# A list-scheduled attention pass in which every operation's place comes from a table instead of a formula

## The chip, the cores and the metric

The kernel runs on one core of one Trainium2 chip. The metric is the device time of one execution in microseconds (us). Five engines of the core work side by side, each through its own instructions in order, and wait for each other on semaphores: TensorE (PE in the profile, with its weight loads as PEld), VectorE (DVE), ScalarE (ACT), GpSimd (POOL) and SyncE (SP), which here issues most of the DMA transfers.

## The reference, cut to what matters

The input is four images of 192 channels and 128 x 128 pixels, in float32. Two layers follow each other. The first is a channel attention; the change doesn't touch it. The second is an attention over dilated neighbourhoods:

```python
pe = conv3x3_depthwise(x, pos_w)                    # 192 channels
x = x + pe + pos_b
q, k, v = split(einsum('oc,bchw->bohw', qkv_w, x))  # three groups of 64 channels each
for dil in (1, 2, 3):                               # a group for each dilation, 2 heads of 32 channels
    scores = sum_d(q * k[3x3 neighbours at distance dil]) / sqrt(32)
    attn = softmax(scores over the 9 neighbours)
    out[group] = sum over the 9 neighbours of attn * v[neighbour]
out = einsum('oc,bchw->bohw', proj_w, out)
```

Borders of k and v are reflected.

## The kernel before, in words

The kernel has three stages. A first pass projects the input and convolves it, a middle stage forms the channel attention's small matrices, and `second_pass` (line 740 on) does the rest: the last 1x1 product of the first layer and the whole second layer. The change concerns the second pass alone.

The second pass works on 64 blocks. A block is four image rows (512 pixels) of a pair of images; 32 blocks make one pair. Each block n goes through these steps:

- **Projection** (`plan_h`): six loads (SP, `loads`, lines 790 and 793), then for each of three tiles m three accumulated matmuls (`h_product`, line 803; m = 2 uses half of TensorE's columns), and an eviction by ACT (`h_evict`, line 807) into a ring of 12 rows, `hboth` and `hring2`.
- **Position convolution** (`plan_conv`): the `centre` tap by ACT into PSUM (pool `pa`, one buffer; line 846), seven taps by DVE that accumulate there (`tap`, line 858), the last of which writes `y`; an eighth neighbour by ACT (`moved`, line 870) that POOL adds (`moved_sum`, line 875). The remaining 64 channels go by nine ACT products (`side`, line 882), two accumulating DMAs that POOL issues (`side_rows`, line 894) and two POOL sums (lines 902 and 905).
- **Keys and values** (`plan_kv`): three pairs of products. A pair's first part (line 945) takes two buffers of the PSUM pool `pc`, the second part (line 948) uses half of TensorE's rows; four evictions by ACT (line 958) go to the rings `kring` (12 rows) and `vring` (16 rows), with reflected columns (lines 962 and 963).
- **Scores** (`plan_scores`): for each of three groups a query in PSUM (pool `q`, one buffer; lines 1000 and 1003), three products by DVE with the shifted keys (`prod`, line 1011), and sums over channels by TensorE (`pick_sums`, line 1022, in a quarter of TensorE's columns).
- **Softmax** (`plan_softmax`): `evicted_scores` (1065), `by_pixel` (1072), `top` (1075), `below` (1079), `exponential` (1082), `total` (1086 and 1087), `divide` (1091), a split of the weights into three bfloat16 parts (1095 to 1105), and a DMA transpose (`weights`, 1110) to `e_sb`.
- **Mixing** (`plan_mixed`): for each of 27 pairs of a group g and a neighbour t TensorE spreads the weights over channels (`expand`, line 1146, two PSUM buffers `ex`), DVE multiplies with the shifted values (`term`, line 1152), and POOL adds (`term_sum`, line 1155; 24 of them, since the first term of a group starts the accumulator). Then come the output products (`out_product`, lines 1164 and 1168, again in `pc`), evictions by ACT (line 1171) and stores by SP.

`pc` has two buffers and serves projection, key/value and output products in turn. `hold` says from which operation to which a buffer is in use.

Nothing of this is issued where it is written. Each step calls `Schedule.add` with an engine, a *rank*, a cost and the operations it comes after. `Schedule.order` (line 60 on) then walks through time with these costs: whenever an engine is free, it takes the ready operation of lowest rank. Ranks count in blocks, so `n + 2` is two blocks after the block's own number. On TensorE an operation whose tile shape differs from the last one's costs `CHANGE` more and has `CHANGE_RANK` added to its rank. The result is one fixed order for every engine; the costs live only in this planning, on the chip the engines follow the order and wait where they must. Buffers of a pool are handed on in order of rank as well. In the kernel before, the ranks are formulas in the code, such as `n + 2 + (j + 0.9) / 8` for tap j, and `t0 + (NT * g + t) / 27` for the mixing.

Of the kernel before, what the change touches and what calls it, by code (L numbers as in the profile page):

```python
# [24 lines left out]
RING = 12  # L25
RING_V = 16
SPARE = 3
NT = 9
# [6 lines left out]
class Schedule:  # L35
# [4 lines left out]
    LATENCY, CHANGE, CHANGE_RANK = 0.2, 0.13, 0.05  # L40

    def __init__(self):
        self.ops, self.pools = [], {}

# [10 lines left out]
    def order(self):  # L55
        import heapq

        for (_, bufs), held in self.pools.items():
            held.sort(key=lambda h: (h[0]["rank"], h[0]["seq"]))
            for i, (first, _) in enumerate(held):  # L60
                if i >= bufs:
                    first["after"] += held[i - bufs][1]
                if i and held[i - 1][0] is not first:
                    first["first"].append(held[i - 1][0])
        for op in self.ops:
            op["left"] = len(op["after"]) + len(op["first"])
            for o in op["after"]:
                o["users"].append(op)
            for o in op["first"]:
                o["issued"].append(op)  # L70
        events, ready, free, shape, out = [], {}, {}, None, []
        for op in self.ops:
            ready.setdefault(op["engine"], [])
            free[op["engine"]] = 0.0
            if not op["left"]:
                heapq.heappush(events, (0.0, op["seq"]))

        def release(op, now):
            op["left"] -= 1
            op["ready"] = max(op.get("ready", 0.0), now)  # L80
            if not op["left"]:
                heapq.heappush(events, (op["ready"], op["seq"]))

        while events:
            now = events[0][0]
            while events and events[0][0] <= now:
                seq = heapq.heappop(events)[1]
                if seq >= 0:
                    ready[self.ops[seq]["engine"]].append(self.ops[seq])
            for engine, ops in ready.items():  # L90
                if not ops or free[engine] > now:
                    continue
                change = lambda o: bool(o["shape"]) and o["shape"] != shape
                op = min(ops, key=lambda o: (o["rank"] + self.CHANGE_RANK * change(o), o["seq"]))
                ops.remove(op)
                end = now + op["cost"] + self.CHANGE * change(op)
                shape = op["shape"] or shape
                free[engine] = end
                heapq.heappush(events, (end, -1))
                out.append(op)  # L100
                for o in op["issued"]:
                    release(o, now)
                for o in op["users"]:
                    release(o, end + op["latency"] * (o["engine"] != engine))
        assert len(out) == len(self.ops)
        self.span = max(free.values())
        return out
# [29 lines left out]
class Stage:  # L137


    def __init__(self, ctx, tc, prefix, sbuf, psum, pools={}):  # L140
        self.nc, self.bufs = tc.nc, {**sbuf, **psum}
        self.schedule, self.tiles, self.written, self.readers = Schedule(), {}, {}, {}
        self.pools = dict(pools)
        for n, k in self.bufs.items():
            if n in pools:
                continue
            space = dict(space=bass.MemoryType.PSUM) if n in psum else {}
            self.pools[n] = ctx.enter_context(tc.tile_pool(name=prefix + n, bufs=k, **space))
# [19 lines left out]
    def repeat(self, ring, kind, m, n, size, rank):  # L168

        if n * RB % size:  # L170
            return
        run = lambda: self.nc.scalar.copy(ring[m][:, size : size + SPARE, :], ring[m][:, 0:SPARE, :])
        after = self.written[kind, m, n] + self.readers.get((kind, m, n - size // RB), [])
        self.written[kind, m, n].append(self.schedule.add("ACT", rank, 0.55, (run,), after))
# [20 lines left out]


# [550 lines left out]
def second_pass(tc, x, w2, xv_p, mix1, mix2, biases, v_dram, v2_dram, out):  # L747
# [4 lines left out]
    with ExitStack() as ctx:  # L752
# [9 lines left out]
            dict(xv=xv_p),  # L762
        )
# [13 lines left out]
        for r in hring:  # L777
            nc.gpsimd.memset(r[:, :, 0 : W + 2 : W + 1], 0.0)

# [34 lines left out]
        def plan_h(n):  # L814
            loaded = [
                [add("SP", n - 0.5 + 0.05 * j, 0.1, (loads, n, j, im), latency=6.0) for im in range(2)]
# [3 lines left out]
            for m in range(3):  # L820
                t = n + 0.65 + 0.11 * m
                ops = [
                    add("PE", t + 0.03 * j, 0.86, (h_product, n, m, j), shape=FULL if m < 2 else COLS)
                    for j in range(3)
                ]
# [6 lines left out]
                ev = add("ACT", t + 0.1, 0.7, (h_evict, n, m), [ops[2]])  # L832
                fill("h", m, n, RING, ev)
                repeat(hring, "h", m, n, RING, t + 0.11)
# [72 lines left out]
        def plan_conv(n):  # L907
            prev = first = add("ACT", n + 2, 1.25, (centre, n), latency=0.3)
            for m in range(2):
                read("h", m, n, 0, first)  # L910
            for j, t in enumerate(AROUND[:7]):
                prev = add("DVE", n + 2 + (j + 0.9) / 8, 1.28, (tap, n, t, j == 6), [prev])
# [4 lines left out]
            mv = add("ACT", n + 2.5, 1.2, (moved, n, AROUND[7]))  # L917
            for m in range(2):
                read("h", m, n, 0, mv)
            both = add("POOL", n + 2.9, 2.4, (moved_sum, n), [mv, two])  # L920
            hold("moved", mv, both)
            firsts, sums = {}, []
            for j, ty in enumerate((1, 0, 2)):
                for tx in range(3):
                    sd = add("ACT", n + 2 + 0.3 * j + 0.08 * tx, 0.72, (side, n, ty, tx), firsts.get(ty, [])[-1:])
                    read("h", 2, n, ty - 1, sd)
                    firsts.setdefault(ty, []).append(sd)
                if j:
                    after = [firsts[1][-1], firsts[ty][-1], *sums[-1:]]
                    sums.append(add("POOL", n + 2.25 + 0.3 * j, 1.2, (side_rows, n, ty), after, latency=6.0))  # L930
                    hold("side", firsts[ty][0], sums[-1])
            for tx in (1, 2):
                sums.append(add("POOL", n + 2.95 + 0.02 * tx, 1.28, (side_sum, n, tx), sums[-1:]))
# [33 lines left out]
        def plan_kv(n, y):  # L967
            used = []
            for pair, t in ((0, n + 3), (1, n + 4.4), (2, n + 4.15)):
                a = add("PE", t, 1.72, (kv_product, n, pair, 0), [y[2]], FULL)  # L970
                b = add("PE", t + 0.03, 0.86, (kv_product, n, pair, 1), [a] + y[3], ROWS)
# [3 lines left out]
                for im in range(2):  # L975
                    for e, (kind, g) in enumerate(groups):
                        ev = add("ACT", t + 0.05 + 0.01 * im, 0.6, (kv_evict, n, pair, im, e, kind, g), [b])
                        evs[e].append(ev)
                    hold("pc", a, *(ops[-1] for ops in evs))
                for e, (kind, g) in enumerate(groups):  # L980
# [3 lines left out]
                    bd = add("ACT", t + 0.07, 0.45, (reflect, n, kind, g), evs[e] + evs[e][0]["after"])  # L984
                    written[kind, g, n] = evs[e] + [bd]
                    repeat(ring, kind, g, n, size, t + 0.08)
# [43 lines left out]
        def plan_scores(n, y):  # L1030
            t0 = n + 4.65
            prods, used, picks = [], [], []
            for g in range(NG):
                a = add("PE", t0 + (NT * g + 0.1) / 27, 0.86, (query, n, g, 0), [y[2]], COLS)
                b = add("PE", t0 + (NT * g + 0.11) / 27, 0.86, (query, n, g, 1), [a] + y[3], FULL)
                used += [a, b]
                mine = []
                for ty in range(3):
                    op = add("DVE", t0 + (NT * g + 3 * ty + 0.5) / 27, 1.75, (prod, n, g, ty), [b])
# [4 lines left out]
            for row in range(7):  # L1044
                of = prods[4 * row // 3 : min(4 * row + 3, NG * NT - 1) // 3 + 1]
                op = add("PE", of[-1]["rank"] + (2.5 + 0.1 * row) / 27, 0.86, (pick_sums, n, row), of, QUADS)
# [65 lines left out]
        def plan_softmax(n, picks):  # L1112
            t0 = n + 5.65
            chain = [picks[-1]]

            def then(engine, t, cost, run, shape=None):
                op = add(engine, t0 + t, cost, (run, n), chain[-1:], shape)
# [3 lines left out]
            s = then("ACT", 0.045, 0.6, evicted_scores)  # L1121
            hold("sc", picks[0], s)
            st = then("PE", 0.05, 0.9, by_pixel, FULL)
            hold("s_sb", s, st)
            mx = then("DVE", 0.05, 0.6, top)
            lo = then("DVE", 0.05, 0.6, below)
            hold("sc", st, lo)
            hold("mx", mx, lo)
            then("ACT", 0.1, 0.55, exponential)
            sm = then("DVE", 0.14, 1.3, total)  # L1130
            dv = then("POOL", 0.16, 0.95, divide)
            hold("sm", sm, dv)
            p0 = then("ACT", 0.19, 0.55, part0)
            then("POOL", 0.21, 1.05, rest)
            then("ACT", 0.24, 0.55, part1)
            p2 = then("POOL", 0.26, 1.05, part2)
            hold("e", lo, p2)
            w = then("SP", 0.3, 0.3, weights)
# [44 lines left out]
        def plan_mixed(n, w):  # L1183
            t0 = n + 6.1
            sums, spreads = [], []
            for g in range(NG):
                exs, prev = [], None
                for t in range(NT):
                    u = t0 + (NT * g + t) / 27
                    exs.append(add("PE", u - 0.6 / 27, 0.25, (expand, n, g, t), [w], FULL))  # L1190
                    tm = add("DVE", u + 0.7 / 27, 0.62, (term, n, g, t), exs[-1:])
# [5 lines left out]
                    prev = add("POOL", u + 1.2 / 27, 1.27, (term_sum, n, g, t), [tm, prev])  # L1197
# [5 lines left out]
            for m in range(2):  # L1203
                ops = []
                for g in range(NG):
                    after = [sums[g][1]] + ops[-1:]
                    ops.append(
                        add(
                            "PE",
                            n + 7.25 + 0.07 * m + 0.01 * g,  # L1210
                            0.86,
                            (out_product, n, m, g),
                            after,
                            FULL if m else ROWS,
                        )
                    )
                used += ops
                for e in range(2 - m):
                    ev = add("ACT", ops[-1]["rank"] + 0.02, 0.6, (out_evict, n, m, e), ops[-1:])
                    hold("pc", ops[0], ev)  # L1220
                    st = add("SP", ev["rank"] + 0.02, 0.3, (store, n, m, e), [ev], latency=5.0)
# [154 lines left out]
```

## Time and profile before

| | |
|---|---|
| median of 3 runs | 4564.9 us (4564.49 to 4565.8) |
| the profiled execution | 4564.56 us, of which the span from first to last instruction is 4562.7 us |
| busy share of the span | PE 97%, DVE 86%, ACT 55%, POOL 74% |
| mean granted TensorE clock | 0.987 |
| first sum of the mixing (line 1155) | 1768.9 us |
| last such sum begins | 4548.4 us |
| DMA | 608.93 MB, 133 GB/s on average |

The page cuts the span into 40 slices and gives the busy share of each in tenths:

```profile
PE   9999999899999989999999999999999999999986
...
DVE  7998889755455547899999999999999999999996
ACT  7888888633233345555555555555555555555531
POOL 6777788611111115888989999998998989999897
PEclk9999999999999989999999999999999999999997
```

The first seven slices are the first pass, the next eight the middle stage, and from the fifteenth on the second pass runs. There PE, DVE and POOL are all at eight or nine tenths, ACT at five. A busy share includes the ends of instructions that overlap the next one, so three engines at nine tenths don't say which of them sets the pace. The mixing is the largest part of the second pass in number:

```profile
L1155 POOL TENSOR_TENSOR acc<-acc,term 128x512 f32<-128x512 f32 x1536 | 1977.4, 1289 | 211.9 <-DVE term L1152 135.5
L1152 DVE TENSOR_TENSOR term<-ex,vring 128x512 f32<-128x512 f32 (+2 forms) x1596 | 1007.3, 661 | 65.8 <-PE ex L1146 38.9
L1011 DVE TENSOR_TENSOR prod<-q,kring 128x1536 f32<-128x1536 f32 (+1 forms) x600 | 1008.3, 1686 | 31.7 <-ACT kring L963 13.8
```

After the shapes and the count stand the busy time in us, the mean of one instruction in ns, and the engine's idle time just before them with what ended most of it.

### The profile page before, as it was taken

The numbers are of one execution on the slowest core, as the hardware profiler recorded it, in microseconds if no ns is written. First come the engines' busy times: TensorE is split into PE (matmuls) and PEld (weight loads), VectorE is DVE, ScalarE is ACT, GpSimd is POOL, SyncE is SP. The second block draws the span as 40 slices with busy tenths as digits, with TensorE's granted clock in tenths as the row PEclk, the third lists the DMA queues.
The fourth block names the chain that finished last, engine by engine and source line by source line (L and its number), as shares of the span: only waits on it lengthen the run. The fifth ranks groups of instructions, "written<-read, shape, count | busy, mean of one in ns | idle before, by whom it ended". The sixth has DMA issues, their size and how long they took to land.

```text
span 4562.7 us, 64190 instructions
## 1 busy us (share of the span) xinstructions
PE 4416.8 (97%) x20608; PEld 1602.8 (35%) x20608; DVE 3907.4 (86%) x5556; ACT 2506.2 (55%) x4794; POOL 3354.2 (74%) x3343
## 2 busy tenths in 40 slices
PE   9999999899999989999999999999999999999986
PEld 3333333345544532333333333333333333333321
DVE  7998889755455547899999999999999999999996
ACT  7888888633233345555555555555555555555531
POOL 6777788611111115888989999998998989999897
PEclk9999999999999989999999999999999999999997
DMA  8777787678677734443444443444434444344311
GB/s 271 241 242 232 244 256 242 192 164 178 150 167 169 167 89 97 99 99 97 101 98 93 105 103 91 106 96 101 101 90 108 98 100 101 92 109 99 78 44 28
DMA packets 483951, 608.93 MB, mean 133 GB/s; under 512 B 136528, under 2 KB 318364, under 8 KB 483616
## 3 DMA queue, kind: packets, MB, share of 16 engines
q1 hardware_dynamic: 464160, 504.94, 40.6%
q0 software_dynamic: 19456, 99.89, 11.3%
q8 instruction: 166, 2.72, 0.3%
q14 instruction: 169, 1.38, 0.1%
HBM read 277.72 MB, written 201.33 MB: 105 GB/s over the span
## 4 chain that ended last, share of the span: by engine, by line
PE 71%; DVE 14%; issue 6%; POOL 6%; DMA 2%; ACT 1%; POOLq 0%; SPq 0%; DVEq 0%; ACTq 0%
PE pc L576 11%; PE ph L803 9%; PE pu L293 7%; PE ex L1146 6%; PE sc L1022 6%; DVE prod L1011 5%; DVE term L1152 5%; POOL acc L1155 4%; PE pu L298 4%; PE gram L648 4%; PE po L1168 3%; PE po L1164 3%; PE pkv L945 3%; PE pu L426 2%; PE q L1000 2%
## 5 line engine op out<-in xcount | busy, mean ns | idle before, releaser
L1155 POOL TENSOR_TENSOR acc<-acc,term 128x512 f32<-128x512 f32 x1536 | 1977.4, 1289 | 211.9 <-DVE term L1152 135.5
L1152 DVE TENSOR_TENSOR term<-ex,vring 128x512 f32<-128x512 f32 (+2 forms) x1596 | 1007.3, 661 | 65.8 <-PE ex L1146 38.9
L1011 DVE TENSOR_TENSOR prod<-q,kring 128x1536 f32<-128x1536 f32 (+1 forms) x600 | 1008.3, 1686 | 31.7 <-ACT kring L963 13.8
L363 POOL TENSOR_TENSOR v_True<-v_True,side 128x512 f32<-128x512 f32 (+1 forms) x512 | 647.9, 1267 | 168.8 <-ACT side L352 141.1
L340 DVE SCALAR_TENSOR_TENSOR pa<-vboth,dwv,pa 128x1024 f32<-128x1024 f32 (+1 forms) x448 | 574.3, 1282 | 76.8 <-ACT pa L333 54.3
L1146 PE MATMUL ex<-e_sb,spread 108*128 108x512 bf16 x1728 | 596.2, 387 | 45.2 <-DVE acc L1152 21.3
L858 DVE SCALAR_TENSOR_TENSOR pa<-hboth,posw,pa 128x1024 f32<-128x1024 f32 (+1 forms) x384 | 489.5, 1275 | 59.0 <-ACT pa L846 45.1
L576 PE MATMUL pc<-u,band 64*64 64x508 f32 (+1 forms) x4608 | 517.5, 590 | 1.4 <-ACT ring L322 1.4
L563 POOL COPY band<-band 64x384 f32<-64x384 f32 x192 | 96.7, 504 | 561.3 <-DMA band<-in_bands 484.8
L1022 PE MATMUL sc<-prod,pick 128*32 128x512 f32 x3456 | 484.1, 607 | 4.1 <-DVE e L1079 2.8
L589 DVE BATCH_NORM_STATS2 stats<-pc 128x6 f32<-128x128 f32 x1440 | 303.3, 283 | 141.3 <-ACT conv L585 141.1
L1146 PEld LDWEIGHTS <-spread 108*128 108x128 bf16 x1728 | 149.0, 98 | 723.7 <-issue 692.2
L945 PE MATMUL pkv<-y,wkv 128*128 128x512 f32 x768 | 389.0, 618 | 8.1 <-ACT kring L958 2.5
L882 ACT ACTIVATE side<-hring,posw 128x512 f32<-128x512 f32 x512 | 335.2, 710 | 102.1 <-DMA side<-side 79.8
L803 PE MATMUL ph<-xv,mix 128*128 128x512 f32 (+1 forms) x1024 | 383.4, 606 | 5.4 <-DMA xv<-v_dram 4.9
L585 ACT COPY conv<-pc 128x512 f32<-128x512 f32 x384 | 211.4, 587 | 295.4 <-PE pc L576 288.8
L293 PE MATMUL pu<-xt,wx 128*128 128x512 f32 x768 | 365.3, 612 | 7.6 <-DMA xt<-in_x 7.6
L352 ACT ACTIVATE side<-ring,dwv 128x512 f32<-128x512 f32 (+1 forms) x512 | 350.6, 736 | 15.1 <-POOL v_True L363 14.3
L958 ACT COPY kring<-pkv 64x512 f32<-64x512 f32 x384 | 223.2, 581 | 221.7 <-PE pkv L948 210.5
L576 PEld LDWEIGHTS pc<-u,band 64*64 64x64 f32 x4608 | 188.4, 133 | 302.3 <-issue 282.1
L1171 ACT COPY o<-po 128x512 f32<-128x512 f32 x192 | 106.2, 588 | 304.5 <-PE po L1164 203.8
L958 ACT COPY vring<-pkv 64x512 f32<-64x512 f32 x384 | 223.4, 582 | 45.4 <-PE pkv L948 35.7
(164 smaller groups left out, 5961.0 us busy)
## 6 DMA issues: line engine op xcount, KB each, us to landing
qk_dram<-us SPq DMA_DIRECT2D x192, 512.0 KB
u<-qk_dram SPq DMA_DIRECT2D x384, 256.0 KB
side<-side POOLq DMA_DIRECT2D x124, 768.0 KB, 5.8
xt<-in_x SPq DMA_DIRECT2D x64, 512.0 KB
v_dram<-v_False SPq DMA_DIRECT2D x64, 512.0 KB
xv<-in_x SPq DMA_DIRECT2D x128, 256.0 KB
xv<-v_dram SPq DMA_DIRECT2D x128, 256.0 KB
out<-o SPq DMA_DIRECT2D x128, 256.0 KB
```

Source lines behind the costliest of these rows:

```text
L293: mm(pu, wx[:, mt * 128 : (mt + 1) * 128], tiles["xt", n][:, im, :], start=True, stop=False)
L340: nc.vector.scalar_tensor_tensor(by_row(to[:, o : o + length]), by_row(vboth[:, at : at + length, :, t % 3 : t % 3 + W]), dwv[:, 0, t : t ...
L363: nc.gpsimd.tensor_add(v[:, rows, :], v[:, rows, :], z[:, rows, :])
L576: nc.tensor.matmul(pcs[e][r * G : (r + 1) * G, :, to], band[at, e, c, dx, :], u[at, e, c, :].rearrange("p (b w) -> p b w", w=W)[:, :, of], ...
L803: mm(to, w[:, cols], tiles["xv", n, j, im], start=j == 0, stop=j == 2)
L858: nc.vector.scalar_tensor_tensor(by_row(to[:, o : o + length]), by_row(hboth[:, at : at + length, :, t % 3 : t % 3 + W]), posw[:, 0, t : t ...
L945: mm(rows3(tile_of("pc", key)), w, tiles["y", n, im], start=True, stop=False)
L1011: nc.vector.tensor_mul(to[:, :, px].rearrange("p t (r w) -> p t r w", w=W), q.unsqueeze(1).to_broadcast([128, 3, *q.shape[1:]]), three,)
L1022: mm(sc[quad * 32 : (quad + 1) * 32, :], pick[:, QR - 4 * row : QR - 4 * row + 32], tiles["prod", n, k // NT, k % NT // 3][:, k % 3, :], s ...
L1146: mm(rows3(tile_of("ex", ("ex", n, g, t))), spread[:, t, :], e_sb, start=True, stop=True)
L1152: nc.vector.tensor_mul(rows3(to[:, px]), rows3(ex[:, px]), win)
L1155: nc.gpsimd.tensor_add(tiles["acc", n, g], tiles["acc", n, g], tiles.pop(("term", n, g, t)))
```

## The change

The formulas go. A table `PLACES` gives each kind of operation a first place and a step; `at(name, n, k)` returns `n + first + step * k`. The costs that the planning uses are set to other values, and for this pass the shape change is planned at 0.10 with a rank penalty of 0.1706 instead of 0.13 and 0.05; the first pass keeps its own. The operations, their dependencies and the buffers' numbers stay as they are. Repeats of ring rows and reflected columns take their rank from the eviction that they follow, plus 0.01.

```diff
+    def __init__(self, change, change_rank):
         self.ops, self.pools = [], {}
+        self.change, self.change_rank = change, change_rank
...
-                op = min(ops, key=lambda o: (o["rank"] + self.CHANGE_RANK * change(o), o["seq"]))
+                op = min(ops, key=lambda o: (o["rank"] + self.change_rank * change(o), o["seq"]))
...
-                end = now + op["cost"] + self.CHANGE * change(op)
+                end = now + op["cost"] + self.change * change(op)
...
+PLACES = {
+    "loads": (-0.2109, 0.00560),
+    "h_product0": (1.0969, 0.01426),
+    "h_product1": (1.8424, 0.03214),
+    "h_product2": (1.7312, 0.00974),
...
+    "centre": (2.2851, 0),
+    "tap": (2.7828, 0.31320),
...
+    "kv0": (4.0938, 0.03845),
+    "kv1": (5.4569, 0.00533),
+    "kvev1": (5.5798, 0.01886),
+    "kv2": (4.8847, 0.03932),
+    "kvev2": (5.2090, 0.00243),
+    "query0": (5.2152, 0.00011),
+    "prod0": (5.3133, 0.08249),
...
+    "pick": (5.5573, 0.12348),
...
+    "weights": (5.7310, 0),
+    "expand": (7.0773, 0.03703),
+    "term": (7.1436, 0.03704),
+    "term_sum": (6.8037, 0.03704),
+    "out0": (8.2271, 0.00732),
...
+}
...
+            (0.10, 0.1706),
...
+        def at(name, n, k=0):
+            first, step = PLACES[name]
+            return n + first + step * k
...
-                prev = add("DVE", n + 2 + (j + 0.9) / 8, 1.28, (tap, n, t, j == 6), [prev])
+                prev = add("DVE", at("tap", n, j), 1.19, (tap, n, t, j == 6), [prev])
...
-                    op = add("DVE", t0 + (NT * g + 3 * ty + 0.5) / 27, 1.75, (prod, n, g, ty), [b])
+                    op = add("DVE", at(f"prod{g}", n, ty), 1.67, (prod, n, g, ty), [b])
...
-                    exs.append(add("PE", u - 0.6 / 27, 0.25, (expand, n, g, t), [w], FULL))
-                    tm = add("DVE", u + 0.7 / 27, 0.62, (term, n, g, t), exs[-1:])
+                    k = NT * g + t
+                    exs.append(add("PE", at("expand", n, k), 0.22, (expand, n, g, t), [w], FULL))
+                    tm = add("DVE", at("term", n, k), 0.60, (term, n, g, t), exs[-1:])
...
-                    prev = add("POOL", u + 1.2 / 27, 1.27, (term_sum, n, g, t), [tm, prev])
+                    prev = add("POOL", at("term_sum", n, k), 1.277, (term_sum, n, g, t), [tm, prev])
```

The other operations of the pass are changed in the same manner. How the instructions then stand on an engine follows only from running the planning, so the prediction reads it from the two built programs.

## The prediction

> **What bounds the kernel now.** I read, in this order, the page's groups, the table of windows, the answer for the accumulating line by stage, the DVE timeline of one block, the waits, and the chain of waits; then how the instructions stand in both programs.
>
> The accumulating line gives the pace, because each block has 24 of its sums:
>
> ```profile
> L1155 POOL TENSOR_TENSOR acc<-acc,term x230: 1259/1276/1583, 1768.9 to 2198.9; 128x512 f32<-128x512 f32 x115
> ...
> L1155 POOL TENSOR_TENSOR acc<-acc,term x1175: 1260/1277/1735, 2198.9 to 4338.8; 128x512 f32<-128x512 f32 x196
> ...
> L1155 POOL TENSOR_TENSOR acc<-acc,term x133: 1259/1270/1767, 4338.8 to 4548.4; 128x512 f32<-128x512 f32 x133
> ```
>
> The counts share their end rows, so there are 229, 1174 and 132 steps: 9.5 blocks at 45.1 us, 48.9 at 43.75, and a tail of 5.5 at 38.1. Before the tail that is 58.5 blocks in 2569.9 us, 43.93 each. Around them lie 1769 us ahead of the first sum, which the change hardly touches, and 14 us behind the last.
>
> Three engines are nearly full in that stage:
>
> ```profile
> core 0: us, PE busy (x) PEld busy (x) DVE busy (x) ACT busy (x) POOL busy (x), PEclk, DMA share, GB/s
> 3000.00:3200.00 200.00, 196.81 (x782) 63.49 (x782) 194.65 (x252) 106.22 (x219) 179.59 (x145) 1.00 0.40 95
> ```
>
> Busy time overlaps at the ends of instructions, so I count from one start to the next. The DVE timeline, from a block's last tap on (the tap itself is left out):
>
> ```profile
> 3057.86 1.28 DVE L1152 TENSOR_TENSOR term<-ex,vring 128x512 f32<-128x512 f32 x2
> 3059.66 1.29 DVE L858 SCALAR_TENSOR_TENSOR pa<-hboth,posw,pa 128x1024 f32<-128x1024 f32 x1 [0.51 <-ACT pa L846]
> 3061.27 0.69 DVE L1152 TENSOR_TENSOR acc<-ex,vring 128x512 f32<-128x512 f32 x1 [0.33 <-PE ex L1146]
> ...
> 3064.88 1.28 DVE L858 SCALAR_TENSOR_TENSOR pa<-hboth,posw,pa 128x1024 f32<-128x1024 f32 x1
> 3066.07 1.28 DVE L1152 TENSOR_TENSOR term<-ex,vring 128x512 f32<-128x512 f32 x2
> 3067.26 1.75 DVE L1011 TENSOR_TENSOR prod<-q,kring 128x1536 f32<-128x1536 f32 x1
> 3068.93 1.28 DVE L1152 TENSOR_TENSOR term<-ex,vring 128x512 f32<-128x512 f32 x2
> ```
>
> A tap takes 3066.07 - 3064.88 = 1.19 us, two terms 1.19, a product 3068.93 - 3067.26 = 1.67. The softmax's four, read off the same timeline, take 0.63, 0.53, 0.98 and 0.37. A block is 27 terms x 0.598 = 16.15, 9 products x 1.67 = 15.0, 7 taps x 1.19 = 8.3 and 2.5: **42.0 us of DVE work**. So DVE stands for 43.75 - 42.0 = 1.75 us in each block. The rows show most of it: the first tap, due at 3057.86 + 1.19 = 3059.05, starts 0.6 late behind ACT's centre; the first term of a group is 0.4 late behind its expand; two more of about 0.2 are in the same block. The waits say that this is so in every block, and that PE's weight loads stand too, for buffers that ACT empties:
>
> ```profile
> PEld pkv L945 <- ACT kring L958: 80.4, 93, 0.9
> ...
> DVE pa L858 <- ACT pa L846: 22.6, 48, 0.8
> ...
> DVE acc L1152 <- PE ex L1146: 14.2, 43, 0.6
> ```
>
> PE's work is in the chain:
>
> ```profile
> 3014.21 0.22 PE ex L1146
> 3014.43 0.99 PE sc L1022 x8
> ...
> 3017.77 1.06 PE pkv L948 x4
> 3018.83 0.32 PE ex L1146
> ```
>
> An expand is 0.22, 0.32 when another tile shape follows. A full-width fp32 product is 0.86; a row of pick sums 0.99, a half-height key/value part 1.06. So leaving the full shape costs 0.10, leaving the picks 0.13, the half-height 0.20; the half-width, 1.01 for a query part in the same chain, 0.15. Without changes a block is 27 x 0.216 + 37.75 products of 0.86 (6.75 pick rows, 9 key/value, 9 projection, 6 query, 6 output, 1 transposing) = 38.3 us.
>
> **The change part by part.** No operation is added or removed; the first pass keeps its order. Only the order within the second pass moves.
>
> *Shape changes.* Counted in PE's order, 1837 become 1533. A block leaves the full shape 12.8 times before and 10.7 after, the picks 6.9 and 5.1, the half-width 4.9 and 4.1, the half-height 4.2 both times: 12.8 x 0.10 + 6.9 x 0.13 + 4.9 x 0.15 + 4.2 x 0.20 = 3.75, and 3.2 after. PE's work falls from 42.0 to 41.5. The Trainium skill has a rule here: TensorEngine Tiling (Array Packing), Key Properties, says that changing the tiling mode drains TensorE; with the fixed part of a warm matmul, about 166 ns (TensorE: Matmul & The Clock Gate, Single matmul latency), I estimate 4.75 x 0.166 = 0.79 us a block, where the rows give 0.55. I take the rows. Either way I book nothing directly: PE is then under DVE's 42.0.
>
> *The stall behind the centre.* Now only two terms (1.2 us) stand between a block's last tap and the next one's first, and the centre takes 1.22 plus hand-overs. In the new DVE order a term, the total with its reciprocal, two products and two terms stand there: 0.6 + 1.35 + 3.3 + 1.2 = 6.5 us. The 0.6 goes. Next late there is ACT itself, by 6.5 - 1.4 = 5 us.
>
> *The expand at the group's start.* It stood behind a 1.72 us key/value product. Now the 0.88 us transposing product stands there: from the term that frees the buffer PE needs 0.22 + 0.88 + 0.38 = 1.5, and DVE has 0.6 + 1.67 + 0.6 = 2.9 to do. The 0.4 goes.
>
> *Do other loops of expand and term close slower?* An expand needs the term two before it, a term its expand. I summed PE's work from one expand to another and DVE's from there to the term that frees the first one a block later. In the old steady order the longest sum is 42.7, above DVE's own work; with 0.35 of hand-overs (0.16 from PE's end, 0.13 and 0.05 from DVE's) 43.05. It's a check that blocks 11 to 19 give 44.7 and 42.4 in turn, and the trace has 45.7 and 41.2 there. In the new order sums over four blocks are 41.95, no more than DVE's own work (single blocks reach 43.3, and the next ones have the room). So these loops stop deciding.
>
> *POOL.* A sum that follows another one of the same accumulator starts 1.355 us after it, otherwise 1.235. The order has 15.6 such pairs a block, now 16.0. With 8.9 us of other work, moves of 0.1 and the DMA issues (0.61 to the next start) POOL needs 40.3 to 41.2: still below 42.0. The two side DMAs and the sums behind them shift in POOL's queue but land in 5.8 us as before; SP's queue is the same but for one transpose moved two places, so loads and stores keep their places. Packing DVE and POOL closer has a rule against it: SBUF — State Buffer, Who interferes with whom, has an exclusive port, taken by a DVE instruction with two SBUF inputs. The pass's two-tensor DVE instructions take one input from PSUM, so by the rule the price is 0. The rows differ a little: a sum takes 1288 ns at 3000 to 3400 and 1265 at 4500 to 4540, where DVE is half idle. I take the rows: 24 x 0.023 = 0.55 us, already in 40.3, with room above it.
>
> *A wait that is added.* ACT's eviction into the third value ring now waits for DVE in 59 of 64 blocks (2 before; a key eviction's wait, 60 times, goes to 3). Behind it in ACT's queue stand the next key evictions, and PE's next key/value product needs the buffers. From the term it waits for: two evictions at 0.605, hand-overs 0.2, product 1.72, expand 0.38 = 3.5 us. DVE has a tap, two terms and two products = 5.7. It is covered, with 2.2 us of room; without cover it costs what exceeds that.
>
> *Drain.* After the last product 74 terms remain instead of 62; POOL adds them at 1.355 while DVE alone would have taken 0.6: 12 x 0.755 = 9 us back.
>
> *Sum.* Bounds: no stall left, 42.0, gives 58.5 x 1.93 = 113 less 9; all stalls left gives 0 less 9. The two largest stalls have covers of over 1 us, so I stay near the first: 42.5 us, 0.5 kept for the smaller hand-overs and the uneven first ten blocks. 58.5 x (43.93 - 42.5) = 84, less 9 = 75. The profiled execution took 4564.6 (span 4562.7), the median is 4564.9: 4490.
>
> **Rivals.**
>
> DVE at its limit (68%): 42.1 to 42.9 a block, 4467 to 4514, likeliest **4490**.
>
> PE stays the bound (22%): its stand-still of 43.75 - 42.0 = 1.75 for ACT's buffers stays, because the same two buffers serve key/value, projection and output; only the shape changes come off. For it: the 80.4 us of waits in that row. Against it: those are weight loads, which partly hide. 58.5 x 0.55 = 32, less 9: 4542.
>
> Slower (6%): the new ACT wait. If ACT reaches the value eviction late, held by its waits on POOL (the longest there now is 4.6 us), each block loses what goes over 2.2 us. It turns the forecast into a loss from 3.5 us on; at 4.6 a block is 42.5 + 2.4 = 44.9, and the time 4564.6 + 57 + 9 = 4630. Against it: ACT is 54% busy.
>
> No change (4%): the order is other, but the pace falls back on something that both share, 4565.
>
> Range: from 4455 (no stall, tail a little shorter) to 4545, which holds the first two. About 0.2%, 9 us, is what a measurement can tell from no change: faster 0.90, same 0.04, slower 0.06.
>
> **What would show it.** Right: 42.1 to 42.9 us between a block's first sums, DVE 98 to 99% of a window, the wait of the tap for the centre gone, PE with more free time than DVE. Wrong: waits of DVE on expands over 1 us a block, ACT's value evictions waiting long for DVE with key/value products late behind them (PE the bound), or a tail more than 10 us longer.

## The result, and the profile after

| | before | changed |
|---|---|---|
| median | 4565.35 us (4 runs, 4564.49 to 4569.99) | 4488.72 us (4 runs, 4487.29 to 4494.03) |
| profiled execution | 4564.56 us, span 4562.7 | 4494.03 us, span 4492.3 |

The ratio is 0.9832, with a 95% interval of 0.9815 to 0.9849: the change makes the kernel 77 us, or 1.7%, faster. The forecast was 4490. The profiled execution of the changed kernel is the slowest of its four, 5 us above their median; sums over its trace are made against 4494.

The accumulating line has moved from L1155 to L1216 (61 lines down, 54 of them the table). By stage, from three answers for that line:

```profile
L1216 POOL TENSOR_TENSOR acc<-acc,term x239: 1251/1275/1571, 1771.5 to 2199.9; 128x512 f32<-128x512 f32 x120
...
L1216 POOL TENSOR_TENSOR acc<-acc,term x1201: 1259/1275/1763, 2199.9 to 4339.4; 128x512 f32<-128x512 f32 x172
...
L1216 POOL TENSOR_TENSOR acc<-acc,term x98: 1260/1268/1288, 4339.4 to 4478.4; 128x512 f32<-128x512 f32 x98
```

There are 238, 1200 and 97 steps. Ahead of 4339.4 that makes 59.9 blocks in 2567.9 us, 42.86 each, but 1.4 of them belong to what was the tail before. Counted to the same sum in both traces, the 1405th, where 58.5 blocks are done (4340.1 us before, 4282.5 now), a block takes 43.95 us before and 42.92 now: 58.5 x 1.03 = 60 us less. The last 5.5 blocks take 195.9 us where they took 208.2, 12 us less. The first sum is 2.6 us later. 60 + 12 - 2.6 = 70, the difference of the two spans.

From here on, the pace of a block is the mean from the first sum of block 10 to that of block 58, counted in 24 sums each: 43.74 us before, 42.88 in the changed kernel.

In the table of windows all three engines are fuller (PE, PEld, DVE, ACT and POOL busy, clock, DMA share, GB/s):

```profile
3000.00:3200.00 200.00, 198.85 (x807) 67.15 (x806) 198.81 (x267) 109.67 (x223) 186.92 (x152) 1.00 0.43 104
```

DVE went from 194.65 to 198.81 of 200 and POOL from 179.59 to 186.92. That looks like the forecast, DVE at its limit. The waits of POOL say something else. Before, from 2200 to 4300 us:

```profile
POOL acc L1155 <- DVE term L1152: 107.9, 68, 3.3
...
POOL y L902 <- DMA side<-side: 6.4, 11, 2.9
```

and after, in the same window:

```profile
POOL y L963 <- DMA side<-side: 51.3, 34, 7.9
POOL e L1161 <- ACT parts L1157: 14.4, 32, 1.1
...
POOL acc L1216 <- DVE term L1213: 1.2, 3, 0.5
```

The columns are the total in us, the times and the longest. Before, POOL waited 108 us for DVE's terms, so it had time to spare. Now it waits 1.2 us for them: POOL is no longer behind DVE. It waits 51 us, 34 times in 49 blocks, for a side transfer, which it hardly did before (6.4 us, 11 times). An engine that has stopped waiting for the others' work is the one to suspect, and the experiments below follow that.

### The profile page after: what moved, and what is told of

Its sections match the earlier page's. It is cut to its first block, busy times and chain, and to the rows that moved or that the text cites. A ratio compares the mean times of both kernels' runs of the same rounds, so it can differ in the third digit from the quotient of the medians.

```text
span 4492.3 us, 64130 instructions
## 1 busy us (share of the span) xinstructions
PE 4364.0 (97%) x20608; PEld 1628.8 (36%) x20608; DVE 3881.9 (86%) x5556; ACT 2514.8 (56%) x4794; POOL 3356.8 (75%) x3343
## 3 DMA queue, kind: packets, MB, share of 16 engines
q0 software_dynamic: 19456, 99.89, 11.5%
## 4 chain that ended last, share of the span: by engine, by line
PE 76%; POOL 9%; DVE 5%; DMA 4%; issue 4%; ACT 1%; POOLq 0%; SPq 0%; DVEq 0%; ACTq 0%
PE pc L635 11%; POOL acc L1216 7%; PE pu L352 7%; PE ph L867 7%; PE sc L1085 7%; PE ex L1207 7%; PE pkv L1006 6%; PE pu L357 4%; PE gram L707 4%; DMA side<-side 3%; PE po L1225 3%; PE pkv L1009 3%; PE q L1066 3%; PE po L1229 3%; PE q L1063 3%
## 5 line engine op out<-in xcount | busy, mean ns | idle before, releaser
L1216 POOL TENSOR_TENSOR acc<-acc,term 128x512 f32<-128x512 f32 x1536 | 1989.1, 1298 | 85.0 <-DVE term L1213 4.6
L1074 DVE TENSOR_TENSOR prod<-q,kring 128x1536 f32<-128x1536 f32 (+1 forms) x600 | 997.4, 1676 | 23.5 <-ACT kring L1024 14.9
L1207 PE MATMUL ex<-e_sb,spread 108*128 108x512 bf16 x1728 | 576.3, 387 | 38.2 <-DVE term L1213 26.5
L1085 PE MATMUL sc<-prod,pick 128*32 128x512 f32 x3456 | 469.2, 602 | 5.0 <-DVE prod L1074 5.0
L1006 PE MATMUL pkv<-y,wkv 128*128 128x512 f32 x768 | 370.4, 603 | 8.6 <-ACT vring L1019 7.7
L867 PE MATMUL ph<-xv,mix 128*64 128x512 f32 (+1 forms) x1024 | 363.9, 594 | 0.5 <-DMA mix<-mixed 0.5
```

Of the source, the lines that this page charges most:

```text
L867: mm(to, w[:, cols], tiles["xv", n, j, im], start=j == 0, stop=j == 2)
L1006: mm(rows3(tile_of("pc", key)), w, tiles["y", n, im], start=True, stop=False)
L1074: nc.vector.tensor_mul(to[:, :, px].rearrange("p t (r w) -> p t r w", w=W), q.unsqueeze(1).to_broadcast([128, 3, *q.shape[1:]]), three,)
L1085: mm(sc[quad * 32 : (quad + 1) * 32, :], pick[:, QR - 4 * row : QR - 4 * row + 32], tiles["prod", n, k // NT, k % NT // 3][:, k % 3, :], s ...
L1207: mm(rows3(tile_of("ex", ("ex", n, g, t))), spread[:, t, :], e_sb, start=True, stop=True)
L1216: nc.gpsimd.tensor_add(tiles["acc", n, g], tiles["acc", n, g], tiles.pop(("term", n, g, t)))
```

## The experiments

All times are compared with the kernel before on the same chip; a ratio stands with its 95% interval. A difference from the changed kernel is one of medians that were not measured side by side; taken from the two ratios instead, it comes out within 4 us of the figure given. The labels beginning with a are edits of the changed kernel, those with b edits of the kernel before.

**Cutting work in the changed order.** Each of three edits shortens one engine's instructions and leaves the order of all engines as it is; each leaves out the part of the computation that its expectation names.

```diff
 # a_dve, in tap
+            im = slice(0, 1) if t == 7 else slice(0, 2)
...
-                    by_row(hboth[:, at : at + length, :, t % 3 : t % 3 + W]),
...
+                    by_row(hboth[:, at : at + length, im, t % 3 : t % 3 + W]),
...
 # a_pe, in h_product
+                px = slice(0, 256) if j == 1 and m < 2 else slice(0, PX)
+                mm(to[:, px], w[:, cols], tiles["xv", n, j, im][:, px], start=j == 0, stop=j == 2)
 # a_pool, in moved_sum
+            y, z = tiles["y", n][:, :, 0, :], tiles.pop(("moved", n))[:, :, 0, :]
+            nc.gpsimd.tensor_add(y, y, z)
```

> The changed kernel in its own order, but one of the seven taps (the fifth) works on one image instead of two, so that part of the convolution is left out. That takes 0.53 us of DVE work from each of 64 blocks and nothing from PE or POOL. If DVE at its limit sets the pace: 64 x 0.53 = 34 us less than the changed kernel, near 4455. If PE sets it: within 5 us of 4489. If POOL's waits for the side transfers set it: at most 10 us less.

Measured: 4491.1 us, ratio to before 0.9833 (0.9818 to 0.9847), the same as the changed kernel. The cut gave nothing. The trace shows where most of it went (DVE's waits from 2200 to 4300). In the changed kernel:

```profile
DVE term L1213 <- PE ex L1207: 14.4, 24, 2.4
DVE term L1213 <- POOL acc L1216: 7.4, 17, 1.0
```

and with the cut:

```profile
DVE term L1214 <- PE ex L1208: 28.7, 54, 2.1
DVE term L1214 <- POOL acc L1217: 12.7, 22, 1.0
```

DVE does less and waits more. It wasn't the engine that sets the pace.

> The changed kernel in its own order, but two of the nine projection products of a block (the middle ones of the two full tiles) cover 256 of 512 columns, so that part of the projection is left out. That takes 2 x 0.43 = 0.86 us of PE work from each block and nothing from DVE. If PE sets the pace: 55 us less, near 4434. If DVE sets it: 0 to 15 us less, by the few waits for expands that are left (20 us in 49 blocks).

Measured: 4486.7 us, 0.9824 (0.9809 to 0.9838): 2 us of 55, within the intervals of both. PE isn't it either.

> The changed kernel in its own order, but POOL adds the moved neighbour for one image of two, so that part of the convolution is left out. That takes about 1.1 us of POOL work from each block. If POOL sets the pace: 70 us less, near 4419. If DVE sets it: 0 to 15 us less, the part of the waits behind the side transfers that POOL's spare time then takes up.

Measured: 4466.3 us, 0.9778 (0.9762 to 0.9794), 22 us less than the changed kernel. That's neither of the two numbers. A block falls from 42.88 to 42.38 us, which is half of the 1.1 us taken out; then something else, 0.5 behind, takes over. POOL sets the pace, with little distance. The trace of this run has POOL waiting for DVE's terms again, 20.9 us, and DVE's own waits from 2200 to 4300 add up to 11 us where they were 30: what takes over is DVE. A cut of ACT's work was not tried.

**POOL's wait alone.** The edit moves one thing on POOL: the sum that first uses the side transfers (L963) stands three POOL instructions later, and the sum after it behind it where it stood in between.

```diff
...
+            two = sums[n, 2]
+            rest = [o for o in ops[ops.index(op) + 1 :] if o["engine"] == "POOL" and o is not two]
...
+            ops.remove(op)
+            ops.insert(ops.index(rest[self.late]), op)
...
+        stage.late = 3
```

> The changed kernel in its own order, with one thing moved: on POOL the first user of the side transfers (the sum of a block's three side rows, with the sum after it where that stands next) stands three POOL instructions later, so that a transfer has eight to ten us to land instead of six. The cuts of DVE and of PE work gave nothing, that of POOL work a third of its size. New theory: POOL sets the pace of the changed kernel, by its own 41 us a block and 1.3 us of waiting for the transfers, with DVE at 42.0 close behind. Then the wait goes and DVE takes over at 42.1 to 42.5: 48 to 58 blocks x 0.4 to 0.8 us, 20 to 45 us less than the changed kernel, 4445 to 4470. If the wait lies in time that POOL has to spare, so that something else sets the pace: within 8 us of 4489.

Measured: 4456.6 us (5 runs, 4455.55 to 4457.78), 0.9758 (0.9744 to 0.9771): 32 us less than the changed kernel, the fastest version here. POOL's waits in it:

```profile
POOL acc L1238 <- DVE term L1235: 45.6, 82, 1.8
...
POOL y L985 <- DMA side<-side: 1.3, 1, 1.3
```

The wait for the transfer is gone, and POOL is behind DVE again. Its window is the one I had forecast for the change:

```profile
3000.00:3200.00 200.00, 199.53 (x812) 67.78 (x806) 199.51 (x269) 113.39 (x228) 186.28 (x150) 1.00 0.43 105
```

DVE is busy 199.5 of 200, and a block takes 42.29 us, against 42.0 of DVE work; from 2200 to 4300 DVE waits 8 us in all. So the change's order holds DVE at its limit once POOL's wait is out of it. The transfer itself isn't faster: it still lands a median of 6.5 us after its issue.

**The same by planning.**

```diff
-                    sums.append(add("POOL", at(f"side_rows{ty}", n), 0.9, (side_rows, n, ty), after, latency=6.0))
+                    sums.append(add("POOL", at(f"side_rows{ty}", n), 0.9, (side_rows, n, ty), after, latency=8.0))
```

> The changed kernel, planned with 8 us instead of 6 from a side transfer's issue to its landing; nothing else is edited. In the changed kernel the second side transfer lands a median of 6.5 us after its issue, its first user stands four sums behind it, and POOL waits for it 51 us in 49 blocks. If these waits, handed on to DVE through the term buffers, are most of what DVE still stands: the waits go and the time falls by 20 to 45 us, to 4445 to 4470. If they lie in POOL's spare time: within 10 us of 4489, or more by what else the planning moves.

Measured: 4509.3 us, 0.9869 (0.9852 to 0.9885), 21 us more than the changed kernel. This doesn't test the wait: POOL still waits for the transfers 42.9 us, 36 times. The planning answers a new latency with another order everywhere. The first sum comes at 1785.4 us instead of 1771.5, and the first ten blocks take 44.5 us each instead of 43.2, while the later ones take 42.67 instead of 42.88.

**The stall at the centre.** One edit puts it back into the changed order, the other takes it out of the old one. Both move only a block's first tap within DVE's order, earlier or later.

> The changed kernel with one thing put back: a block's first tap stands one DVE instruction (a term) behind the last tap of the block before, so that it waits for ACT's centre. The centre takes 1.22 us and about 0.35 of hand-overs, the term 0.6: DVE stands for 0.95 us more in each block. If DVE sets the pace and the covered stall was worth its length: 64 x 0.95 = 60 us more, near 4549. If the stall at the centre was not what the old order lost time by, because DVE had time to spare: within 10 us of 4489.

Measured: 4585.3 us, 1.0041 (1.0027 to 1.0056), 97 us more than the changed kernel, and more than either forecast. DVE's two longest waits there:

```profile
DVE prod L1089 <- PE sc L1100: 43.3, 47, 1.9
DVE pa L934 <- ACT pa L922: 34.5, 47, 1.0
```

The tap waits 0.73 us a block for the centre, and a product, 0.9 us a block, for a product buffer that PE's pick sums free; that second wait isn't in the changed kernel. Together that is the size of the 1.6 us by which a block is longer (44.49 against 42.88). In this order the cover is worth more than the stall's own length.

> The kernel before with one thing moved: a block's first tap stands behind two more terms, so that the centre has 2.4 us of cover instead of 1.2 and the wait for it goes. If that stall of 0.6 us was a loss of its own: 64 x 0.6 = 38 us less, near 4527. If the first term behind it was late because PE's expand came late anyway, the wait only moves from the tap to the term: the same or up to 40 us more.

Measured: 4615.2 us, 1.0103 (1.0088 to 1.0118), 46 us more, a little over the second forecast. DVE's waits from 2200 to 4300 before:

```profile
DVE pa L858 <- ACT pa L846: 21.8, 47, 0.5
DVE acc L1152 <- PE ex L1146: 13.9, 42, 0.6
```

and with the tap moved:

```profile
DVE acc L1167 <- PE ex L1161: 86.8, 41, 2.1
...
DVE pa L873 <- ACT pa L861: 0.8, 5, 0.2
```

The tap's wait for the centre has gone from 21.8 us to 0.8, and the first term's wait for its expand has grown from 13.9 to 86.8. In the old order that tap stood in time in which the expand hadn't come yet: the stall at the centre was no loss of its own.

**What set the old pace.** The same cuts of DVE and PE work in the old order:

> The kernel before in its own order, with the same cut of one tap (0.53 us of DVE work a block; part of the convolution is left out). If loops through PE and DVE set the old pace, the cut counts in them: 64 x 0.53 = 34 us less, near 4531. If PE alone set it: within 5 us of 4565.

Measured: 4558.2 us, 0.9976 (0.9967 to 0.9984): 11 us of 34, neither of the two numbers.

> The kernel before in its own order, with the same cut of two projection products (0.86 us of PE work a block; part of the projection is left out). If loops through PE and DVE set the old pace: between 15 and 55 us less, by how much of the loop runs on PE where the products stand. If PE alone set it: 55 us less, near 4510. If DVE's own stalls at the centre set it, without PE: within 5 us of 4565.

Measured: 4551.4 us, 0.9963 (0.9950 to 0.9976): 18 us of 55. Both cuts count, each for a third. That speaks for loops that run through both engines, and against either alone; how they share isn't settled, and no cut of POOL's or ACT's work was tried in the old order.

**Which part of the change.** The planned price of a shape change alone, the new costs alone, and the table with the old costs:

```diff
 # b_shape
+        stage.schedule.CHANGE, stage.schedule.CHANGE_RANK = 0.10, 0.1706
 # b_costs: before's ranks; one of its lines
-                prev = add("DVE", n + 2 + (j + 0.9) / 8, 1.28, (tap, n, t, j == 6), [prev])
+                prev = add("DVE", n + 2 + (j + 0.9) / 8, 1.19, (tap, n, t, j == 6), [prev])
 # a_oldcosts: the table; one of its lines
-                prev = add("DVE", at("tap", n, j), 1.19, (tap, n, t, j == 6), [prev])
+                prev = add("DVE", at("tap", n, j), 1.28, (tap, n, t, j == 6), [prev])
```

> The kernel before with its own rank formulas and costs, but with the planned price of a shape change of the changed kernel (0.10, rank penalty 0.1706). PE's order has 1581 shape changes instead of 1837 (the changed kernel has 1533): 256 x 0.12 = 31 us less PE work. If the fewer shape changes carried the gain: 31 us or more less, below 4535. If they are booked at nothing, as I did: 4565 within 15 us, either way, by what else the other order moves.

Measured: 4616.05 us, 1.0105 (1.0090 to 1.0120), outside both forecasts. With 256 of the 304 shape changes gone, the time is 47 us more. The fewer changes don't carry the gain by themselves; what costs here is the other order that came with them, in which DVE waits 58 us for POOL to free term buffers (0.8 before), and POOL 93 us for side transfers (6.4 before).

> The kernel before with its rank formulas, planned with the changed kernel's costs (shape change 0.10, rank penalty 0.05 as before). If the durations from records carried the gain, because the planning then sees where DVE would stand: about 4490 to 4510. If the table of places carries it: 4550 to 4580. PE's order has 1873 shape changes, more than before.

Measured: 4550.9 us, 0.9960 (0.9945 to 0.9975): 16 us less, a fifth of the gain.

> The changed kernel's table, planned with the old costs (shape change 0.13, rank penalty 0.1706). If the places carry the gain: 4490 to 4520. If they only work with the durations that they were searched with, because ready times decide more than ranks: 4530 or more.

Measured: 4665.0 us, 1.0214 (1.0199 to 1.0229), 176 us more than the changed kernel. A block takes 46.1 us. The same places with other planned durations give another order, the slowest one measured. The gain is neither in the costs nor in the places; it belongs to the pair. POOL's wait for the side transfers is long in both of these orders too, 86 us in b_costs and 128 in a_oldcosts, from 2200 to 4300. Moving their first user there was not tried.

## Why the prediction was right, and where it was right by luck

**The total.** 4490 was forecast, 4488.7 came. In the sum two terms were off and nearly cancelled: I had 84 us from the blocks and 9 back in the drain; the trace has 60 from the blocks and 12 gained in the drain, which so had the wrong sign. That they met so close to the forecast is luck.

**The blocks.** "DVE at its limit (68%): 42.1 to 42.9 a block" has 42.88 at its end, but DVE was not what set it: a_dve took out 34 us of DVE work and gained nothing. The signs that I had named for it came nearly all the same: the pace, the tap's wait gone, DVE busy 99% of the window. They can't tell a kernel that DVE sets from one in which DVE follows closely behind POOL. Only the sign on PE failed: it has no more free time than DVE (198.85 us busy of 200 against 198.81). The step that failed is POOL's: "POOL needs 40.3 to 41.2: still below 42.0", with side DMAs that "land in 5.8 us as before". POOL's own work was sized well: 42.88 less its waits of 1.83 (51.3 + 14.4 + about 24 us of smaller ones, over 49 blocks) is 41.05. The waits weren't in the sum at all. With the longest of them out of the way (a_ss_late), a block takes 42.29 us, of which DVE waits 0.16: its work, put at 42.0, was sized well too. The POOL timeline of the changed kernel shows one wait for a transfer:

```profile
3048.26 0.87 POOL L955 DMA_DIRECT2D side<-side  x1
3048.87 5.62 POOL L1216 TENSOR_TENSOR acc<-acc,term 128x512 f32<-128x512 f32 x4
3056.66 1.28 POOL L963 TENSOR_TENSOR y<-side 128x512 f32<-128x512 f32 x1 [2.17 <-DMA side<-side]
```

Issue, four sums, then the first user: a cover of 0.61 + 5.6 = 6.2 us, which would have held a landing of 5.8. Here it landed about 8.4 us after its issue. Landing times before, and in the changed kernel, both from 2200 us on:

```profile
DMA to landing us min/median/max: 5.5/5.8/8.1
...
DMA to landing us min/median/max: 5.5/6.5/14.1
```

I looked at the order of POOL's and SP's queues and took the old landing time for granted, though the new order puts the issue elsewhere in time: in this block it follows the softmax's transpose, issued at 3047.1, by 1.2 us. That is so in the trace at large. From 2200 to 4300 us a transpose is issued within 1.5 us of a block's second side transfer in 47 of 49 blocks, and those transfers land in 6.5 to 14.1 us; the two without one land in 5.5 and 5.6. Before, no transpose came so near, and the second transfers took 5.5 to 6.4. a_oldcosts has both in one run: 11 with a transpose that near took 6.7 to 11.5 us, 35 without took 5.6 to 6.4. So the longer landing goes with the transpose beside it. That the transpose causes it was not tested by an edit that moves it alone.

**The two stalls.** They went, as forecast. The tap stands after 6.4 us of other work (6.5 were forecast), without a wait:

```profile
3034.36 1.28 DVE L919 SCALAR_TENSOR_TENSOR y<-hboth,posw,pa 128x1024 f32<-128x1024 f32 x1
...
3041.99 1.28 DVE L919 SCALAR_TENSOR_TENSOR pa<-hboth,posw,pa 128x1024 f32<-128x1024 f32 x1
```

But "The 0.6 goes" booked it as a loss of its own, and b_tap_late shows that in the old order it wasn't: PE's expand was late behind it anyway. The loops of expand and term, which I summed beside it, were the better account of the old pace; b_dve and b_pe agree with them in kind.

**Shape changes.** Booked at nothing, because PE stood under DVE. b_shape doesn't settle that, since another order came with it. In the changed order a_pe agrees: 0.86 us less PE work a block gave 2 us. In the old order the same cut gave 18 (b_pe), so the 0.55 us of the fewer changes may have been worth some 0.55/0.86 x 18 = 12 us of the gain; that is an estimate.

**The added wait** of ACT for DVE is there, 29.7 us in 35 cases, and DVE's waits for expands, 0.4 us a block (14.4 + 5.5 us in 49 blocks), leave little that could stand behind it: right. The slower rival that hung on it didn't come.

**PE as the bound** (22%) is ruled out by a_pe.

**The drain.** I priced 12 more terms at POOL's pace against DVE's. The tail's blocks took 38.1 us before, more than POOL's 24 x 1.355 + 2.84 = 35.4 for sums and softmax, so POOL wasn't the limit there; now the last ones take 34.5 to 35.8. My price assumed the old tail to be at a limit that it hadn't reached. What held the old tail wasn't tried.

## What to carry to other kernels

When an order is packed until three engines have within 3% the same work, their busy shares no longer say which sets the pace. Here it was the one that waited in its own queue for a transfer that the sum had left out. Look for the engine that no longer waits for the others, and test it by cutting its work with the order held fixed. A stall that a row shows is only a loss if what comes behind it is ready: move the stalled instruction alone and see whether the wait moves with it. In this list schedule places and planned durations worked only as a pair; moving one or two instructions of a block in the finished order gave 32 us, where re-planning with a longer latency lost 21.

## What the runs showed of the hardware that was not expected

The side transfers, nearly all of 768 KB and issued in the same way, land in 5.8 us in the old order and 6.5 in the new one (medians), with single ones of 14.1, though the core's DMA share is 0.40 and 0.43. Moving their user left the 6.5 as it was. Over all 14 traces, from 2200 to 4300 us, the second transfers of a block with a softmax transpose issued within 1.5 us of them take 6.3 to 14.1 us (339 of them, median 6.5), those without take 5.5 to 7.6 (337, median 5.7).
